# A two-layer outlook-attention kernel: the row shifts of layer 0 move behind the last third of the logits, and some jobs move by a slot

## The chip, the cores and the metric

The kernel runs on one core of one Trainium2 chip. The metric is the device time of one execution in microseconds (us). About 0.3% of it, some 10 us, can be told from no change.

## What is computed

The input `x` is [8, 56, 56, 384] in float32: 8 images of 56 x 56 positions with 384 channels. Two layers follow each other, each of the form x + conv(group_norm(x)). Cut to what matters, layer 0 is:

```python
v = einsum('bhwc,oc->bhwo', x, Wv)                       # values
a = einsum('bhwc,oc->bhwo', x, Wa).reshape(b, n, 12, 9, 9)
attn = softmax(a * 32 ** -0.5, axis=-1)                  # 12 heads, 9 x 9 weights a position
out = einsum('bnhpq,bnqhd->bnphd', attn, v_unf)          # v_unf: the 3 x 3 neighbours of v
...                                                      # each of the 9 outputs is added to its
y = canvas[:, pad:pad + h, pad:pad + w]                  # own neighbour position
return einsum('bhwc,oc->bhwo', y, Wo)
```

Layer 1 is simpler: 6 heads, one set of 9 weights a head and position (with biases), a softmax over the 9, the weighted sum over the 3 x 3 neighbours, and an output projection.

## The kernel before, in words

Images go in pairs (4 pairs, 112 rows of two images side by side on the partitions), and within a pair by image columns (56). Layer 0 runs one column a step, 4 x 56 = 224 steps and 3 more to drain. The instruction order on every engine is written by hand: what Python emits first runs first on its engine.

A step of `layer0` calls `attend(pair, c, between)`. It multiplies the normalised tokens by the attention weights in three thirds (`project`, PSUM tiles called `bank`, TensorE); after each third VectorE takes the maximum (`mx`) and subtracts it (into `at`), and then `between(n)` is called with n = 0, 1, 2. After the thirds come the exponential on ScalarE, the projection to the values `v` (TensorE, copied out by ScalarE) and `between(3)`. The 8 columns of a block are packed into 7 full tiles of 128 tokens; so in every eighth step (step % 8 == 7, where `j == NTILE`) there are no logits, and `attend` only calls `between(0)` to `between(3)`, one after another.

`between` is where all else of the step is put:

- `turning`: TensorE transposes of the next pair's input (`pt`), a ScalarE copy and VectorE statistics.
- `weigh()`: for the column before, the softmax sums on VectorE and the division on POOL (`at<-at,den`); for the column before that, `presum`, which adds the overlapping weights of three neighbouring columns into `pre` (POOL, and two ScalarE copies at n = 3); then the values go to a table in HBM (`vtab`, POOL's DMA queue). In the block's last steps `share_out` spreads the eighth column's weights over DMAs (`last<-at`, `at<-last`, `at<-at`).
- `folding`: `fold` for the column three steps back, in two parts. The first part prepares weight tiles `wts`: VectorE memsets, two ScalarE scalings for each of one or two patches, two TensorE matmuls with a shift matrix (`pw<-pre,shift`), which move rows of `pre` up and down, and a VectorE addition of `pw` and `pre` into `wts` for each patch. The second part issues two DMAs a patch on SyncE (`ztab<-wts`) that write `wts` to a table in HBM.
- `jobs.run(step, 1)`: takes one job from a queue, if the head of the queue is due.

The jobs are made by `fetch`, once in 7 steps for a patch of 7 columns: it loads the table of weights into `z` (one tile for each of the two images, SyncE) and adds ten jobs with the due step `step + 4`: four contractions (two for each image: each does 48 matmuls of a 121-row table with 32 columns, PSUM tile `pc` in two buffers, and ScalarE copies them to `yT`), and six output projections (`po`, one PSUM buffer; VectorE adds the residual into `x1t`). For the last patch of a pair three more jobs follow, the parts of `norm_params` for layer 1: `bn_aggr` on VectorE, the group means (`pgmean`, TensorE), the group variances (`pgvar`). The queue is first in, first out, and a job that is not yet due holds back all behind it. Jobs run at n = 0 and n = 2, and in every eighth step at n = 3 too.

SyncE's DMA queue is in order as well: in a step it holds the table writes of `fold`, then (from `upkeep`) `xT<-xt`, `xr<-in_x`, `xin<-xT`, then (from `flush`) `last<-at`, `at<-last`, `x<-x1t`, `xres<-xT`, and then `vp<-vtab` and `z<-ztab` of `fetch_v` and `fetch`.

The helpers `matmul` and `InOrder` emit every operation, so the profile shows L119 for matmuls, L122 for transposes and L134 for most others; the tile names tell them apart.

Of the kernel before, what the change touches and what calls it, by code (L numbers as in the profile page):

```python
# [15 lines left out]
def two_outlook_layers(  # L16
# [101 lines left out]
    def matmul(*args, **kwargs):  # L118
        tc.keep_in_program_order(nc.tensor.matmul(*args, **kwargs))  # L119
# [26 lines left out]
    def projected(name):  # L146
        return patch.tile([P, NCH, PX, IMG, H], F32, tag="yT", name=f"yT_{name}", bufs=1)
# [195 lines left out]
    def bands(queue, z, table, line, slot, row, top, groups, b, py, npy):  # L343

        for (s0, s1), (m0, m1) in groups:
            first = (b * H + top) * line + s0 * slot + m0 * row
            queue.dma_start(
                z[s0:s1, :, m0 * row : m1 * row],
                bass.AP(
                    table.tensor, table.offset + first + bands.at[row],  # L350
                    [[slot, s1 - s0], [py * line, npy], [1, (m1 - m0) * row]],
                ),
            )
# [19 lines left out]
    NC = 2  # L373
# [10 lines left out]
    jobs = Jobs()  # L384
    later = []

    def flush():
        while later:
            later.pop(0)()
# [21 lines left out]
    def project_half(po, w, yT, half, j):  # L411
        lo, hi = HALVES[half]
        for i in range(NCH):
            matmul(
                po[:, : (hi - lo) * R],
                w[:, i, j * P : (j + 1) * P],
                yT[:, i, lo:hi].rearrange("p m b y -> p (m b y)"),
                start=(i == 0), stop=(i == NCH - 1),
            )

    def layer0(late, pools):
# [342 lines left out]
        def load_res(pair, px):  # L764

            xres[pair, px] = late_w.tile([P, NCH, T], F32, tag="xres", name=f"xres_{pair}_{px}")
            later.append(
                lambda: sync.dma_start(xres[pair, px], xTs[pair][:, :, px * T : (px + 1) * T])
            )

        def fetch(pair, px, due):

            nm = f"0_{pair}_{px}"
            n_tile = 2
            yT = projected(nm)
            if not pair and not px:
                load_res(0, 0)
            for b in range(IMG):
                z, vp = zs[b], vps[b]
                bands(  # L780
                    sync, z, ztab0[(pair * NPX + px) % NTAB], LINE0, SLOT0, ROW0, 0, GROUPS0,
                    b, PY0, NPY0,
                )

                def contract(t, b=b, z=z, vp=vp):
                    pc = ps.tile([P, NCH, n_tile, PY0, PX], F32, tag="c", name=f"pc_{nm}_{b}_{t}", bufs=NC)
                    for n in range(n_tile):
                        py = t * n_tile + n
                        zp = z[: SX0 * SY0, py].rearrange("s (y h m) -> s y h m", y=PY0, h=HEADS0)
                        for h in range(HEADS0):  # L790
                            i, j = divmod(h, P // D0)
                            matmul(
                                pc[j * D0 : (j + 1) * D0, i, n],
                                vp[: SX0 * SY0, py, h * D0 : (h + 1) * D0],
                                zp[:, :, h, :],
                                start=True, stop=True,
                            )
                    rows_of = slice(t * n_tile * PY0, (t + 1) * n_tile * PY0)
                    scalar.copy(
                        yT[:, :, :, b, rows_of], pc.rearrange("p i n y m -> p i m (n y)")  # L800
                    )

                for t in range(0, NPY0 // n_tile, NC):
                    jobs.add(due, lambda t=t, f=contract: [f(t + n) for n in range(NC)])
            if pair == NPAIR - 1 and px == NPX - 1:
                jobs.add(due, clear_bands)
            if px == 0:
                st1s[pair] = stat.tile([P, NCH, IMG, 2 * NPX, 6], F32, tag="st1", name=f"st1_{pair}")

            def project_out(half, j):  # L810
                lo, hi = HALVES[half]
                n = (hi - lo) * R
                po = ps.tile([P, 4 * R], F32, tag="o", name=f"po_{nm}_{half}_{j}")
                project_half(po, wo_t, yT, half, j)
                if j == 0:
                    fetch.x1t = late_w.tile([P, NCH, 4, R], F32, tag="x1t", name=f"x1t_{nm}_{half}", bufs=2)
                x1t = fetch.x1t
                vector.tensor_tensor(
                    x1t[:, j].rearrange("p m r -> p (m r)")[:, :n], po[:, :n],
                    xres[pair, px][:, j, lo * R : hi * R], ALU.add,  # L820
                )
                for b in range(IMG):
                    vector.bn_stats(
                        st1s[pair][:, j, b, 2 * px + half, :],
                        x1t[:, j, : hi - lo, b * H : (b + 1) * H],
                    )
                if j == NCH - 1:
                    later.append(
                        lambda: sync.dma_start(
                            x1s[pair][px, :, :, lo * R : hi * R],  # L830
                            x1t.rearrange("p i m r -> p i (m r)")[:, :, :n],
                        )
                    )
                    if half:
                        del xres[pair, px]
                        following = divmod(pair * NPX + px + 1, NPX)
                        if following[0] < NPAIR:
                            load_res(*following)

            for half in range(2):  # L840
                for j in range(NCH):
                    jobs.add(due, lambda half=half, j=j: project_out(half, j))
            if px == NPX - 1:
                def params_part(n):
                    if n == 0:
                        making["1"] = norm_params(st1s.pop(pair), f"1_{pair}", params1, pair)
                    next(making["1"])

                for n in range(3):
                    jobs.add(due, lambda n=n: params_part(n))  # L850

        making = {}
        clearing = list(clears())
# [47 lines left out]
        for step in range(NPAIR * W + LAG):  # L901
            folding = fold(*divmod(step - LAG, W)) if step >= LAG else iter(())
            turning = turned(step)
            summing = []

            def weigh():

                normal = 1 <= step < NPAIR * W + 1 and (step - 1) % SB < NTILE
                if normal:
                    normalise(*divmod(step - 1, W))  # L910
                if normal and step % SB == NTILE:
                    share_out(*divmod(step - 1, W))
                if 2 <= step < NPAIR * W + 2:
                    summing.append(presum(*divmod(step - 2, W)))
                    next(summing[0])
                if normal and step % SB < NTILE:
                    share_out(*divmod(step - 1, W))
                if normal:
                    keep_v(*divmod(step - 1, W))

            def between(n):

                if n == 0:
                    next(turning, None)
                    weigh()
                    jobs.run(step, 1)
                elif n == 1:
                    next(folding, None)
                    next(turning, None)
                elif n == 2:  # L930
                    jobs.run(step, 1)
                else:
                    for part in summing:
                        next(part)
                    next(folding, None)
                    if step % SB == NTILE:
                        jobs.run(step, 1)

            if step < NPAIR * W:
                attend(*divmod(step, W), between)  # L940
                upkeep(step)
            else:
                for n in range(K + 1):
                    between(n)
            flush()

            pair, c = divmod(step - LAG - PX, W)
            if pair >= 0 and c % PX == 0:
                fetch_v(pair, c // PX)
            pair, c = divmod(step - LAG - PX - 1, W)  # L950
            if pair >= 0 and c % PX == 0:
                fetch(pair, c // PX, step + 4)
# [336 lines left out]
```

## Time and profile before

| | |
|---|---|
| median of 4 runs | 3481.6 us (3475.37 to 3491.45) |
| the profiled execution | 3475.37 us |
| its span, first to last instruction | 3473.5 us |
| TensorE busy, instructions | 3228.6 us, 28510 |
| layer 0 | about the first 2260 us |
| mean granted TensorE clock | 0.965 |
| DMA | 859.13 MB, mean 247 GB/s |

The profile has these views: the busy time of each engine over the span, and in stretches of it (with the granted clock of TensorE and the share of time that the 16 DMA engines were busy); the waits, which say for each engine what it was idle before and whose work ended that idleness; and the timeline of instructions. In a timeline line the number after the start is the duration, x6 is the number of instructions that ran without a gap, and the bracket gives the idle time before the group and what ended it. A float32 matmul stands as two instructions. "issue" is a wait whose end no semaphore in the profile explains.

### The profile page before, as it was taken

To read this page: it belongs to the slowest core of one execution; us is meant where nothing else is said; L and a number is where in the kernel's file an instruction comes from. 1 tells how busy PE (TensorE), PEld (TensorE's weight loads), DVE (VectorE), ACT (ScalarE), POOL (GpSimd) and SP (SyncE) were. 2 spreads that over 40 slices of the span, in tenths; PEclk is the share of its full clock that TensorE was granted. 3 is DMA by queue.
4 is the path that set the end of the run, shared out by engine and by line. 5 is a ranking of instruction groups with operands and counts; after the bars stand their busy time and mean duration, and the time that the engine had idled before them with its cause. 6 is when DMAs were issued, how large, how long until landed. Compare 5 with 4: busy or idle time off the path is not lost.

```text
span 3473.5 us, 74347 instructions
## 1 busy us (share of the span) xinstructions
PE 3228.6 (93%) x28510; PEld 2202.3 (63%) x28510; DVE 1872.6 (54%) x4780; ACT 1368.6 (39%) x3755; POOL 1366.9 (39%) x1982
## 2 busy tenths in 40 slices
PE   7688999999999999999999999888999999999998
PEld 5456676666666666667666666645666666666665
DVE  5556766676777676676666767532333333333231
ACT  4333444344444344443433443323434333433432
POOL 2544545555445454455454555422222222222220
PEclk7899999999999999999999999989999999999998
DMA  6788988888888787879766868768787878787875
GB/s 194 225 286 288 317 278 267 278 277 268 295 278 284 231 278 265 290 260 309 246 198 219 297 227 270 259 225 225 209 227 213 235 212 229 216 221 217 230 211 141
DMA packets 595753, 859.13 MB, mean 247 GB/s; under 512 B 205798, under 2 KB 470950, under 8 KB 591302
## 3 DMA queue, kind: packets, MB, share of 16 engines
q1 hardware_dynamic: 476806, 682.87, 62.4%
q0 software_dynamic: 59136, 148.12, 13.4%
q10 hardware_dynamic: 59456, 23.40, 2.9%
q8 instruction: 224, 3.67, 0.5%
q14 instruction: 131, 1.07, 0.1%
HBM read 520.28 MB, written 330.40 MB: 245 GB/s over the span
## 4 chain that ended last, share of the span: by engine, by line
PE 36%; DMA 7%; issue 3%; DVE 2%; ACT 1%; POOL 1%; SPq 1%; POOLq 0%; DVEq 0%; ACTq 0%
PE bank L119 18%; PE po L119 10%; PE pc L119 5%; DMA at<-lgtab 3%; DMA lgtab<-lgt 1%; DMA ztab<-wts 1%; PE pw L119 1%; PE pt L122 1%; ACT xn L134 1%; PE bank L122 1%; SPq L134 1%; DMA z<-ztab 1%; DMA vtab<-v 0%; POOL at L134 0%; DMA vp<-vtab 0%
## 5 line engine op out<-in xcount | busy, mean ns | idle before, releaser
L119 PE MATMUL bank<-wa_t,xn 128*128 128x288 f32 x3528 | 983.1, 417 | 9.2 <-ACT xn L134 6.1
L119 PE MATMUL po<-yT,wo_t 128*128 128x448 f32 (+1 forms) x2304 | 828.0, 499 | 26.2 <-DVE x1t L134 23.6
L134 POOL TENSOR_TENSOR at<-at,den 128x972 f32<-128x972 f32 x196 | 440.3, 2247 | 930.2 <-DVE den L134 533.9
L119 PEld LDWEIGHTS bank<-wa_t,xn 128*128 128x128 f32 x3528 | 658.8, 194 | 225.7 <-issue 26.2
L119 PEld LDWEIGHTS po<-yT,wo_t 128*128 128x128 f32 x2304 | 429.2, 192 | 316.2 <-issue 188.2
L134 ACT ACTIVATE at<-at 128x972 f32<-128x972 f32 (+1 forms) x228 | 215.3, 944 | 974.0 <-DVE at L134 973.0
L332 POOL DMA_DIRECT2D vtab<-v x392 | 213.1, 547 | 844.1 <-DVE v L134 799.0
L119 PE MATMUL bank<-wc_t,xn 128*128 128x438 f32 x1176 | 480.8, 545 | 0.0
L134 DVE TENSOR_REDUCE mx<-bank 128x36 f32<-128x324 f32 x588 | 284.9, 484 | 350.3 <-PE bank L119 346.8
L119 PE MATMUL pc<-z,vp 121*32 121x49 f32 (+1 forms) x17664 | 385.5, 221 | 62.8 <-ACT yT L134 28.9
L119 PEld LDWEIGHTS pc<-z,vp 121*32 121x32 f32 (+1 forms) x17664 | 346.3, 123 | 133.8 <-issue 84.0
L119 PE MATMUL bank<-wv_t,xn 128*128 128x384 f32 x1176 | 423.7, 497 | 0.0
L134 DVE TENSOR_TENSOR at<-bank,mx 128x324 f32<-128x324 f32 x588 | 291.3, 495 | 170.1 <-ACT pre L134 59.1
L119 PEld LDWEIGHTS bank<-wc_t,xn 128*128 128x128 f32 x1176 | 215.3, 192 | 170.5 <-issue 163.8
L119 PEld LDWEIGHTS bank<-wv_t,xn 128*128 128x128 f32 x1176 | 222.8, 193 | 137.2 <-issue 15.3
L134 POOL DMA_DIRECT2D vtab<-v x476 | 289.5, 612 | 21.8 <-DMA vtab<-zeros 11.1
L134 ACT COPY yT<-pc 128x294 f32<-128x294 f32 (+2 forms) x512 | 196.4, 405 | 244.6 <-PE pc L119 242.8
L134 POOL TENSOR_TENSOR pre<-at,at 112x108 f32<-112x108 f32 (+1 forms) x440 | 224.1, 526 | 92.6 <-DMA at<-last 62.0
L134 DVE SCALAR_TENSOR_TENSOR x1t<-po,bo_t,x1t 128x448 f32<-128x448 f32 (+1 forms) x156 | 97.6, 626 | 249.0 <-PE po L119 249.0
L134 DVE TENSOR_TENSOR lgt<-bank,ba_t 128x54 f32<-128x54 f32 x196 | 41.7, 213 | 348.0 <-PE bank L119 348.0
L134 ACT COPY ot<-pt 112x384 f32<-112x384 f32 x128 | 61.3, 479 | 382.2 <-PE pt L122 341.5
L134 ACT ACTIVATE xn<-xin,bias,scale 128x168 f32<-128x168 f32 (+1 forms) x474 | 208.4, 504 | 3.1 <-DMA xin<-xT 3.1
(113 smaller groups left out, 3075.3 us busy)
## 6 DMA issues: line engine op xcount, KB each, us to landing
z<-ztab SPq DMA_DIRECT2D x64, 2352.0 KB
vp<-vtab SPq DMA_DIRECT2D x64, 1536.0 KB
vp<-vtab SPq DMA_DIRECT2D x64, 945.0 KB
xres<-xT SPq DMA_DIRECT2D x32, 1176.0 KB
ztab<-wts SPq DMA_DIRECT2D x336, 110.2 KB
vtab<-v POOLq DMA_DIRECT2D x108, 336.0 KB, 6.3
xin<-xT SPq DMA_DIRECT2D x52, 672.0 KB
xr<-in_x SPq DMA_DIRECT2D x50, 672.0 KB
```

Of the source, the lines that this page charges most:

```text
L119: tc.keep_in_program_order(nc.tensor.matmul(*args, **kwargs))
L122: tc.keep_in_program_order(nc.tensor.transpose(*args, **kwargs))
L134: return lambda *args, **kwargs: tc.keep_in_program_order(op(*args, **kwargs))
L332: queue.dma_start(bass.AP(table.tensor, table.offset + first, [*([line * step, count] for step, count in rows_of or ((1, rows),)), *([[(R ...
```

## The change

```diff
                 for t in range(0, NPY0 // n_tile, NC):
-                    jobs.add(due, lambda t=t, f=contract: [f(t + n) for n in range(NC)])
+                    jobs.add(due + b, lambda t=t, f=contract: [f(t + n) for n in range(NC)])
...
                 for n in range(3):
                     jobs.add(due, lambda n=n: params_part(n))
+                    if n < 2:
+                        jobs.add(due, lambda: None)
...
                 elif n == 1:
-                    next(folding, None)
                     next(turning, None)
                 elif n == 2:
                     jobs.run(step, 1)
+                    next(folding, None)
```

Three edits, all in layer 0. The first part of `fold` is emitted in `between(2)` after the job instead of at the start of `between(1)`: behind the last third of the logits and the second job of the step. The contractions of the second image (b = 1) become due one step later than those of the first. And between the three parts of `norm_params` for layer 1 an empty job takes a slot each. No instruction is added or removed; only the order on the engines changes.

## The prediction

> **What bounds the kernel now.** I read the busy shares first. TensorE (PE) is busy for 93% of the span and VectorE, the next engine, for 54%, so a microsecond counts only if TensorE gets it back.
>
> ```profile
> PE 3228.6 (93%) x28510; PEld 2202.3 (63%) x28510; DVE 1872.6 (54%) x4780; ACT 1368.6 (39%) x3755; POOL 1366.9 (39%) x1982
> ```
>
> Then the busy time by stages: layer 0 after its start (440 to 2224 us), one step without a stall, and two stretches with one. The columns are us, busy time of PE, PEld, DVE, ACT and POOL, the granted TensorE clock, and the DMA share with GB/s.
>
> ```profile
> 440.00:2224.00 1784.00, 1695.31 (x16423) 1205.11 (x16422) 1230.29 (x3251) 739.59 (x1986) 898.15 (x1208) 0.98 0.80 264
> 638.80:648.70 9.90, 9.90 (x221) 7.41 (x220) 5.70 (x14) 5.25 (x13) 5.48 (x9) 1.00 0.68 219
> 704.30:717.30 13.00, 10.47 (x133) 7.42 (x128) 3.97 (x12) 5.26 (x15) 6.95 (x12) 0.87 0.92 290
> 1318.00:1336.00 18.00, 12.62 (x354) 10.15 (x355) 7.71 (x23) 7.71 (x23) 12.00 (x19) 0.72 0.80 242
> ```
>
> A normal step keeps TensorE busy throughout at full clock. Idle in the long stretch is 1784.0 - 1695.3 = 88.7 us. What ended it is in TensorE's waits of that stretch (total us, times, longest):
>
> ```profile
> PE pw L119 <- POOL pre L134: 26.4, 10, 3.7
> PE po L119 <- DVE x1t L134: 17.7, 20, 4.0
> PE pc L119 <- issue: 13.5, 13, 2.8
> PE pw L119 <- issue: 9.1, 8, 2.4
> PE pc L119 <- ACT yT L134: 5.7, 5, 1.5
> PE pgmean L119 <- DVE mv L134: 5.6, 6, 1.6
> ```
>
> `pw` is the row shift that the change moves. TensorE's timeline shows where it stalls: in the step after one whose number leaves 7 when divided by 8 (a "boundary step", without logits of its own).
>
> ```profile
> 624.52 0.64 PE L119 MATMUL pw<-pre,shift 112*112 112x120 f32 x4 [0.98 <-issue]
> 625.00 3.18 PE L119 MATMUL bank<-wa_t,xn 128*128 128x288 f32 x12
> 631.89 1.14 PE L119 MATMUL pw<-pre,shift 112*112 112x120 f32 x4 [3.71 <-POOL pre L134]
> 632.83 2.69 PE L119 MATMUL bank<-wa_t,xn 128*128 128x288 f32 x6
> 637.29 1.62 PE L119 MATMUL bank<-wa_t,xn 128*128 128x288 f32 x6
> ```
>
> The reader sees two thirds of logits, a stall of 3.71 us, and then the last third at 2.69 us where the same six instructions take 1.62 otherwise. A stall costs its length and a slow stretch behind it. In a normal step `pre` is finished long before: at 600.7 for the `pw` at 607.8.
>
> **Part 1, the row shift behind the last third and the job.** Nothing is added; 224 folds move. On TensorE each `pw` (4 instructions, 0.58 us) now has 6 logits instructions (1.63 us) ahead of it and, where there is a job, a contraction job (1.45 us) or a projection (1.86 to 2.42 us). The stall shrinks by that cover.
>
> Of the ten waits (26.4 us) the trace puts three (2.48, 2.49, 2.85) into boundary steps without logits or jobs: they stay. Three of 3.7 us are in steps without a job: 1.63 us each is covered, 4.9 us. Four (2.53, 0.96, 2.86, 1.03) have third and job in front, 3.1 us or more: 7.4 us goes. Of the eight waits on "issue" one of 1.1 us stands in a full step and goes; the others are in boundary steps. Sum **13.4 us**. The waits before 440 us (9.06 and 3.24 us the largest) I cost at nothing: TensorE waits there for input as well (11.06 us for `xr` at 317), and what is saved is waited for again.
>
> In a boundary step two jobs become neighbours that had `pw` between them. The second waits for the copy or addition that empties the first one's PSUM, as before, but 0.58 us of `pw` no longer fills that wait. With projections, twelve such waits grow by 0.58 us; the 0.58 us then stands between the second and the third job, where about sixteen waits of some 0.6 us are. I set this at zero (between -9 and +7 us).
>
> **Part 2, second image a step later.** Jobs run two a step and three in a boundary step, so only four windows, whose due step is 15, 71, 127 or 183, change: there the third contraction of that step leaves. Two of those thirds stalled 2.65 us (at 1331.7) and 2.81 us (at 1877), behind ScalarE's copies that wait for POOL. Gain 5.5 us, less 4 x 0.6 us of `pw` now uncovered: **3.1 us**. The contraction itself moves, at no cost.
>
> **Part 3, an empty job after two of the three parts of the norm's parameters.** The group means wait for six `bn_aggr` of 0.53 us; one job slot more (about 5 us) covers them. Three of the four windows lie in layer 0; the rows say 5.6 us plus 1.7 us for the variances. I take **5 us**. The fourth is followed by a wait of 11.3 us for `vp` and counts for nothing. The window has 15 job slots in 7 steps and needs 15, so nothing runs over.
>
> **Part 4, the clock.** A row first: 704.3 to 717.3 has 13 us at 0.87, that is 1.7 us lost after a stall of 2.53 us; 1318 to 1336 loses 18 x 0.28 = 5.0 us. Eleven half-clock stretches stand behind the stalls of parts 1 to 3, 24 us together. Some stalls only shrink, so I take half, **12 us** (0 to 24).
>
> The Trainium skill, "TensorE: Matmul & The Clock Gate", section "Part 1: The HAM clock gate", gives half clock after at least one idle window of about 3.4 us. By it only the three stalls of 3.7 us would trip the gate and, cut to 2.1 us, would stop doing so: three times 1.7, or 5 us, and the sum would be 7 us less. The trace disagrees: the clock fell after 2.53 us of idleness.
>
> **What it costs.** The fold's VectorE adds (0.5 us each) now stand behind the last third's reduction and subtraction (0.49 and 0.49 us) and the job's addition and statistics. In the step of 607 us they ran at 610.7 and would run near 613.8; in the contraction step of 641 us, 1.3 us later. VectorE has room (5.70 us busy of 9.90). But SyncE sits on exactly these adds:
>
> ```profile
> SPq L134 <- DVE wts L134: 469.9, 93, 11.9
> ```
>
> So the two table writes and all that is queued behind them on SyncE start 1.3 to 3 us later: `last<-at`, `x<-x1t`, `xin`, `xr`, `xres`, and `z`. Two of these matter. VectorE waits for `last<-at` ten times (48.6 us), because an `at` buffer is still being read; half of those lie behind 500 us, and one shows through on TensorE as 1.44 us for a bank. Five waits longer by 1.5 us: 8 us. And `z`: from the trace's 2,352-byte packets, the first 1,024 of each 2,048 taken as image 0's, the first contraction starts 1.2 to 16.3 us after them, median about 11; five of the 32 windows have 3.6 us or less. About 1 us each: 4 us. Cost **12 us**, between 0 (all hidden) and 62 (below). ScalarE's two to four scalings (0.6 to 1.0 us together) now come just before the exponential; VectorE needs that a step later, so nothing.
>
> **Sum.** 13.4 + 3.1 + 5 + 12 - 12 = 21.5 us. The profiled execution took 3475.4 us (span 3473.5): 3453.9. The median of the four runs is 6.2 us above the profiled one, which was the fastest; I add that: **3460 us**, 0.6% faster.
>
> **Rivals.**
> *Absorbed.* `pre` is late because POOL is, and what TensorE saves it waits for at the next late thing: `last<-at`, `z`, or the x1t addition (17.7 us now). For it: the stalls before 440 us end in waits for transfers. Against it: TensorE is busy for all of a normal step, and POOL for little over half. Then only parts 2 and 3 stay, 8 us less the 12: about 3480 us.
> *SyncE becomes the bound (slower).* The table writes start 3 us later, SyncE is in order, and `last<-at` and `z` land 3 us later in a queue that is busy to 0.80. If that reaches TensorE in full, ten waits for `at` buffers and five tight `z` windows grow by 3 us, 45 us, and ten of them trip the clock, 17 us: 62 us against a gain of 33.5, so 3510 us; with half of it on TensorE about 3480. It decides from a shift of 3 us, where the tight windows' slack ends. For it: SyncE's 469.9 us. Against it: most windows have over 8 us.
> *More than I count.* All 24 us of the clock come back and SyncE's shift is hidden: 45.5 us, 3436 us; with the early stalls too, 3425.
>
> **How the numbers follow.** Measurement tells 0.3%, about 10 us, from no change. My forecast and its neighbourhood (3445 to 3471) 0.45, more than I count 0.21, absorbed 0.18, SyncE slower 0.16. The likeliest is the forecast, 3460. Faster by over 0.3% is the first two, 0.66; within it 0.18; slower 0.16. The range takes in the larger gain and half of the slower rival: 3422 to 3494.
>
> **What would show it.** Right: the `pw` waits on `pre` between 440 and 2224 fall from 26.4 us to 10 to 15, those left standing in boundary steps and behind them; the two long waits of `pc` go; `pgmean` no longer waits for `mv`; the layer's clock rises from 0.98. Wrong: waits of `bank` for `at`, of `pc` for `z` or of `po` for `x1t` grow by as much, or VectorE's wait for `last<-at` rises well above 48.6 us. A fold that becomes late for `z` in most windows would make the prediction wrong in sign.

## The result and the profile after

The changed kernel takes 3487.84 us (median of 53 runs, 3473.67 to 3503.5) against 3479.78 us for the kernel before (79 runs, 3467.59 to 3493.93). The ratio is 1.0025, 95% interval 1.0018 to 1.0032: slower by 0.25%, where 0.6% faster was predicted. Its profiled execution has a span of 3474.2 us, 0.7 us above that of before. The medians differ by 8.1 us, so one profile of each cannot carry the sign; what it can carry is where the stalls went.

Layer 0 by stages in after, with the columns of the prediction's table. The stretch reaches the same step as the one shown of before, and is 14 us longer:

```profile
440.00:2238.00 1798.00, 1698.61 (x16434) 1211.37 (x16429) 1250.63 (x3254) 742.43 (x1991) 901.92 (x1212) 0.98 0.80 263
```

TensorE's idle time is 1798.0 - 1698.6 = 99.4 us; before it was 88.7 us. The clock is the same 0.98. TensorE's waits of after in this stretch (total us, times, longest):

```profile
PE pc L119 <- ACT yT L134: 15.9, 11, 3.5
...
PE pt L122 <- DMA xr<-in_x: 11.0, 5, 3.5
PE pw L119 <- POOL pre L134: 9.6, 4, 2.8
PE bank L119 <- DVE at L134: 8.6, 6, 2.3
PE pw L119 <- ACT pre L134: 7.4, 5, 2.2
```

Read this list against the one of before. The row shift did what was hoped: `pw` waited 26.4 + 9.1 = 35.5 us and now waits 9.6 + 7.4 and, in two smaller rows, 1.0 + 0.9, together 18.9 us. But other rows grew. `pc<-ACT yT` went from 5.7 to 15.9 us. `pt<-DMA xr` went from 2.5 to 11.0 and `bank<-DVE at` from 2.5 to 8.6. Those three alone give back 24.8 us for the 16.6 saved.

The stall that the prediction showed at 631.9 us stands in TensorE's timeline of after here:

```profile
628.00 4.64 PE L119 MATMUL bank<-wa_t,xn 128*128 128x288 f32 x18
634.89 1.14 PE L119 MATMUL pw<-pre,shift 112*112 112x120 f32 x4 [2.25 <-POOL pre L134]
635.82 3.31 PE L119 MATMUL bank<-wv_t,xn 128*128 128x384 f32 x6
```

The last third now runs without a gap behind the first two (18 instructions in one group), and the stall is 2.25 us instead of 3.71. The slow stretch behind it remains: the values' projection takes 3.31 us, elsewhere 2.10. The stall got shorter, but the clock still fell (0.76 granted from 633 to 640 us).

What the fold's lateness does is seen in the waits of the other engines, over the whole run of after:

```profile
DVE at L134 <- DMA last<-at: 91.4, 22, 13.9
...
ACT xn L134 <- DMA xin<-xT: 18.3, 5, 4.8
```

And SyncE's own waits in after:

```profile
SPq L134 <- DVE wts L134: 637.0, 117, 11.0
```

Before, the first was 48.6 us (10 times), the second 3.1 us (once) and the third 469.9 us (93 times). SyncE stands longer in front of `wts`. Relative to the step, its DMAs start later than before by a median of 2.1 us (`ztab`), 2.0 (`last<-at`), 2.5 (`xr`), 1.4 (`z`) and 2.5 (`vp`). `xin` is hardly late at the median (under 0.4 us); it is late in single steps.

### The profile page after: what moved, and what is told of

Its sections match the earlier page's. It is cut to its first block, busy times and chain, and to the rows that moved or that the text cites. A ratio compares the mean times of both kernels' runs of the same rounds, so it can differ in the third digit from the quotient of the medians.

```text
span 3474.2 us, 74310 instructions
## 1 busy us (share of the span) xinstructions
PE 3218.7 (93%) x28510; PEld 2202.4 (63%) x28510; DVE 1894.3 (55%) x4780; ACT 1370.6 (39%) x3755; POOL 1366.5 (39%) x1982
## 3 DMA queue, kind: packets, MB, share of 16 engines
q1 hardware_dynamic: 476806, 682.87, 62.7%
## 5 line engine op out<-in xcount | busy, mean ns | idle before, releaser
L119 PE MATMUL bank<-wa_t,xn 128*128 128x288 f32 x3528 | 943.3, 415 | 14.8 <-DVE at L134 8.2
L119 PEld LDWEIGHTS bank<-wa_t,xn 128*128 128x128 f32 x3528 | 671.9, 194 | 248.6 <-issue 25.5
L134 DVE TENSOR_TENSOR at<-bank,mx 128x324 f32<-128x324 f32 x588 | 291.3, 495 | 197.8 <-DMA last<-at 91.4
L134 POOL DMA_DIRECT2D vtab<-v x476 | 289.5, 612 | 23.0 <-DMA vtab<-zeros 12.3
L119 PEld LDWEIGHTS bank<-wv_t,xn 128*128 128x128 f32 x1176 | 213.2, 195 | 110.7 <-issue 7.0
L134 DVE TENSOR_TENSOR lgt<-bank,ba_t 128x54 f32<-128x54 f32 x196 | 41.6, 212 | 343.8 <-PE bank L119 343.7
L134 ACT ACTIVATE xn<-xin,bias,scale 128x168 f32<-128x168 f32 (+1 forms) x474 | 208.4, 504 | 18.3 <-DMA xin<-xT 18.3
```

The lines of the kernel that those rows point to most:

```text
L134: return lambda *args, **kwargs: tc.keep_in_program_order(op(*args, **kwargs))
```

## The experiments

Three theories were told apart. **S**: the late tables hold SyncE, and what waits in its queue comes too late. **N**: `pw` used to lie between two jobs and covered the second one's wait for its PSUM tile; now it doesn't. A third place for the loss is the other two parts of the change. All ratios are to the kernel before on the same chip, with 95% intervals. The runs are spread over four chips: e1 to e4 on one, e6 to e9 on a second, e10 to e12, the control and e15 on a third, l1, l2, e13 and e14 on a fourth. Where two kernels of different chips are compared, only their ratios are.

### The three parts, one at a time

`e1_fold` is the fold's move alone.

```diff
                 elif n == 1:
-                    next(folding, None)
                     next(turning, None)
                 elif n == 2:
                     jobs.run(step, 1)
+                    next(folding, None)
```

> The fold's first part behind the last third and the job, alone. Theory S (SyncE is in order and sits on the fold's VectorE adds, so tables and all loads and stores behind them start some 2 us later): 0.1 to 0.5% slower than before, VectorE's wait for last<-at near the 91 us of the changed kernel (before 48.6). Rival P (the row shift's place alone pays, and one of the other two edits loses): 0.5% or more faster.

Measured: 1.0063 (1.0038 to 1.0089), 3487.17 us where the kernel before ran 3459.84. Waits of its whole run:

```profile
DVE at L134 <- DMA last<-at: 76.3, 15, 13.5
...
PE pc L119 <- ACT yT L134: 62.7, 30, 5.2
...
ACT xn L134 <- DMA xin<-xT: 18.0, 5, 5.0
```

The same rows as in after are long, and SyncE's wait for `wts` is 667.4 us. The loss sits in this part.

`e2_due` has only `jobs.add(due + b, ...)` for the contractions.

> The second image's contractions due a step later, alone. S and P's first form: within 0.15% of before, since four windows change; the waits of the third contraction in a boundary step (2.65 and 2.81 us) go. If this edit loses by itself: over 0.2% slower.

Measured: 0.9999 (0.9977 to 1.0021). Alone, this edit has no effect that can be measured.

`e3_params` has only the empty jobs:

```diff
                     jobs.add(due, lambda n=n: params_part(n))
+                    if n < 2:
+                        jobs.add(due, lambda: None)
```

> The two empty jobs between the parts of the norm's parameters, alone. My sum: 5 us (0.15%) faster, no wait of pgmean left. After the changed trace: the group means now come right behind the transposes, whose PSUM tile they share, and wait for the copy xt (5.0 and 4.9 us), so 0 to 0.2% slower.

Measured: 1.0009 (0.9990 to 1.0029). The wait for `mv` that the prediction wanted to remove is gone (`pgmean` for `mv`: 8.0 to 0.4 us over the run), but `pgmean` now waits 6.9 and `pgvar` 5.0 us for ScalarE's `xt`. TensorE's timeline of after shows the same:

```profile
773.79 0.55 PE L122 MATMUL pt<-ident,xr 112*128 112x112 f32 x4
777.43 2.50 PE L119 MATMUL pgmean<-mv,gmat 128*128 128x2 f32 x14 [3.09 <-ACT xt L134]
790.72 2.16 PE L119 MATMUL pgvar<-part,gmat 128*128 128x2 f32 x14 [2.45 <-ACT xt L134]
```

The empty jobs shift `pgmean` and `pgvar` to slots at n = 0. There they stand right behind the transposes `pt`, whose PSUM tile they share, and wait 3.09 and 2.45 us for ScalarE's copy `xt` to empty it. Part 3 traded one wait for another.

The three ratios multiply to 1.0071, the whole change has 1.0025. The intervals of the three together reach to about 0.004 either way, so whether the parts help each other is not settled. The kernel before ran at 3459.84 us on the chip of these runs, 0.6% under its time on the others; whether the fold's move costs more there than elsewhere isn't settled either.

### The second part of the fold

`e4_tables_last` is after with the table writes moved behind the step's other SyncE DMAs, so that no `ztab` stands ahead of `last<-at` and `xin`.

```diff
                     for part in summing:
                         next(part)
-                    next(folding, None)
...
             flush()
+            next(folding, None)
```

> The changed kernel, with the fold's table writes issued on SyncE at the end of the step, behind the step's other loads and stores (still ahead of vp and z). S: VectorE's wait for last<-at falls from 91 to under 50 us, ScalarE's for xin from 18 to under 5, and the time to 0.4 to 1% below before (3445 to 3465). P, or ScalarE's scalings as the cause: unchanged within 0.2% of the changed kernel (3480 to 3492).

Measured: 1.0143 (1.0117 to 1.0170), the second largest ratio of all. Its waits:

```profile
ACT wts L134 <- DMA ztab<-wts: 169.2, 47, 17.6
...
DVE at L134 <- DMA last<-at: 43.7, 14, 13.3
```

The wait for `last<-at` halved (91.4 to 43.7 us) and ScalarE's for `xin` fell from 18.3 to 0.8, as S says, but the time that S expected did not follow. The table writes now left so late that the `wts` buffers were still being read when the next fold wanted them: ScalarE's wait for them went from 17 us in after to 169.2 and VectorE's from 7 to 101.7. The order in one queue can't be mended by exchanging who is late.

### Lateness without the moved row shift

`e6_late_adds` keeps `pw` at its old place and only puts VectorE's additions into `wts` behind the second job. That is S without N.

```diff
+            yield   # ahead of the additions in fold
...
                 elif n == 2:
                     jobs.run(step, 1)
+                    next(folding, None)
```

> The kernel before, with only the fold's VectorE additions (the ones that add pw and pre) moved behind the second job; the row shift on TensorE and ScalarE's scalings stay where they were. Theory S (late table writes hold up SyncE): 0.2 to 0.6% slower, VectorE's wait for last<-at 65 us or more, ScalarE waits for xin. Theory N (the row shift no longer stands between the two jobs of a boundary step, and that is the loss): within 0.15% of before.

Measured: 1.0064 (1.0040 to 1.0087). Its waits:

```profile
DVE at L134 <- DMA last<-at: 95.4, 21, 14.3
...
PE pw L119 <- POOL pre L134: 49.7, 19, 11.0
...
ACT xn L134 <- DMA xin<-xT: 16.0, 5, 5.2
```

And the same rows in a control, the unchanged kernel (`c_before`, with run e10 below):

```profile
DVE at L134 <- DMA last<-at: 54.1, 12, 12.5
...
PE pw L119 <- POOL pre L134: 51.0, 17, 9.1
...
ACT xn L134 <- DMA xin<-xT: 5.3, 1, 5.3
```

The `pw` stalls are as before, nothing is gained, and the two waits for transfers have grown to what they are in after (91.4 and 18.3 us), SyncE's for `wts` from 456.2 to 667.3 us. Lateness of the additions alone costs 0.64%, as much as the whole fold's move (0.63%). Since e1 also saves `pw` stalls (24.2 us on POOL against 49.7) and its ratio is no better, what it saves there is spent elsewhere. The row that is longer in e1 is `pc<-ACT yT` on TensorE, 62.7 us against 38.8.

`e7_before_job` puts the fold behind the last third, but ahead of the job (`next(folding, None)` before `jobs.run(step, 1)` at n = 2).

> The fold's first part behind the last third, but ahead of the second job. In boundary steps the row shift stands between the two jobs again. N: 0.3 to 0.6% faster than before, as the stalls of the row shift shrink by 1.63 us each. S: table writes are late by about a third, so about 1 us: between 0.2% faster and 0.3% slower.

Measured: 0.9995 (0.9977 to 1.0014). Standing one job earlier removes the whole loss. VectorE's wait for `last<-at` is long here too (82.2 us), so that wait by itself isn't what costs; ScalarE's for `xin` is 9.1 us.

`e8_not_in_boundary` is e1, except that in boundary steps (where two jobs would become neighbours) the fold stays in front. `e9_after_boundary_only` moves the fold only in the step after a boundary step, where the stalls of 3.7 us were.

```diff
# e8
                 elif n == 1:
+                    if step % SB == NTILE:
                         next(folding, None)
...
# e9
                 elif n == 1:
+                    if step % SB:
                         next(folding, None)
```

> The fold's first part behind the second job in all steps but the boundary ones, where it stays ahead. N: 0.2 to 0.6% faster than before, no waits of pc of over 2.5 us in boundary steps. S: 0.3 to 0.6% slower, as with the fold's move alone (1.0063).

> The fold's first part behind the second job only in the step after a boundary step (28 of 224), where the stalls of 2.5 to 3.7 us were; early everywhere else. S and N both: the covered stalls (some 13 us and part of their clock) without the costs, 0.2 to 0.6% faster than before. If it isn't faster, the stall only moves, whatever SyncE does.

Measured: e8 1.0048 (1.0026 to 1.0069), e9 1.0021 (1.0003 to 1.0039). In e8 the row shift is back between the jobs of the boundary steps, and most of the loss remains, so N is small: 0.15% between the ratios of e1 and e8, inside both intervals. e9 is the surprise: 28 late folds, all where the large stalls are, and it still doesn't win. A table of its steps (from ScalarE's copy of `v` in one step to that of the next) showed why. Its three largest losses against the control are 5.2, 3.75 and 5.7 us at steps 29, 85 and 141, each 56 steps from the next, and at the fourth of this series, 197, it loses 1.2 us. (The next largest, 3.3 and 3.0 us, are at steps 48 and 51.) The four are the first contraction steps of the windows that load their tables right behind a late fold, at steps 24, 80, 136 and 192 (`vp`), with `z` one step later.

### The mechanism in the timeline

That led to one window of this series, the one contracted from step 85 on, in after (which loses 3.9 us at that step) and before. SyncE's queue in after:

```profile
897.29 1.77 SPq L134 DMA_DIRECT2D ztab<-wts  x4
...
906.38 1.08 SPq L134 DMA_DIRECT2D z<-ztab  x2
...
915.74 2.21 SPq L134 DMA_DIRECT2D xin<-xT  x1
```

The same DMAs in the trace of before:

```profile
885.95 1.80 SPq L134 DMA_DIRECT2D ztab<-wts  x4
...
892.73 1.00 SPq L134 DMA_DIRECT2D z<-ztab  x2
902.32 1.01 SPq L134 DMA_DIRECT2D xin<-xT  x1
```

Steps 81 to 84 lie 8.8 to 6.7 us later in after anyway; `z` goes out 13.65 us later, at the end of step 81, so some 5 us later within its step. The packet records say what follows: the 2,048 packets of `z` (2,352 bytes each) start from 907.4 to 922.5 us, over 15.1 us, and the 1,792-byte packets of the two transfers of transposed input behind them (`xT<-xt` and `xin`) come only at the end and after, 921.7 to 926.5. Before, the packets of `z` started from 893.8 to 908.4, and those behind them from 907.0 to 913.3. Then ScalarE in after:

```profile
927.07 1.59 ACT L134 ACTIVATE xn<-xin,bias,scale 128x168 f32<-128x168 f32 x4 [3.97 <-DMA xin<-xT]
...
928.98 0.69 ACT L134 COPY yT<-pc 128x294 f32<-128x294 f32 x2
```

and TensorE in after:

```profile
929.43 1.44 PE L119 MATMUL pc<-z,vp 121*32 121x49 f32 x96 [2.75 <-ACT yT L134]
```

Read the three together from the bottom. The contraction at 929.43 waits 2.75 us for `yT`. ScalarE copies `yT` at 928.98 because it is in order and stood 3.97 us at `xn`. And `xn` stood for `xin`, which was behind `z` in SyncE's queue. The row that grows on TensorE (`pc<-ACT yT`) thus has nothing in common with the thing that was moved but the queue. In before, `xn` of this step runs without a wait, and no contraction of it waits longer than 0.5 us:

```profile
916.30 1.59 ACT L134 ACTIVATE xn<-xin,bias,scale 128x168 f32<-128x168 f32 x4
```

The same chain stands three more times in after, each 56 steps from the next: at 369 us (ScalarE waits 3.85 us for `xin`, then TensorE 2.88 for `yT`), at 1480 (4.76 and 3.53) and at 2015 (1.10 and 1.16). Together TensorE waits 10.3 us in the four; in before there is none.

### Another queue, an earlier fold, a lighter load

`e10_fold_act_queue` is e1 with `last<-at` and `xin<-xT` issued on ScalarE's queue (`scalar.dma_start` for `sync.dma_start`); `e11_before_act_queue` has the same on the kernel before.

> The fold's move alone, with last<-at and xin issued on ScalarE's DMA queue in place of SyncE's. If SyncE's order does the damage (theory S): VectorE's wait for last<-at and ScalarE's for xin fall back to those of the kernel before or under, and the ratio to the next kernel is 1.000 or under. If the late table writes do it through z alone, or the row shift's place itself: 0.4 to 0.7% above the next kernel.

> The kernel before with the same two transfers on ScalarE's queue. S: 0 to 0.4% faster than before. Rival (ScalarE pays for the issues, 0.6 us each): 0 to 0.5% slower.

> The kernel before, unchanged, for its trace and the width of the comparison on this chip: ratio 1.000 within 0.2%.

Measured: e10 1.0182 (1.0153 to 1.0211), e11 1.0062 (1.0040 to 1.0084), the control 1.0005 (0.9986 to 1.0023). The relief failed. VectorE's wait for `last<-at` and ScalarE's of `xn` for `xin` are gone in e10, but TensorE's wait for `xr` is 100.6 us (control 41.6, e11 59.2), and SyncE's for `wts` 750.1. The fold costs 1.2% there (1.0182 / 1.0062), twice as much as in e1. ScalarE, in order too, is held by the issues: its idle time on "issue" is 21.0 us in e11 and 28.5 in e10 (control 3.3), and in e10 the issues of `xin` and `last<-at` at 922.96 and 923.56 us take 0.56 and 0.59 us. S had said 1.000 or under for this pair, so by what was put down it missed; since the queue change has a price of its own, the miss weighs little.

`e12_early` goes the other way: in steps with 2 <= step % 8 < 7 the fold is emitted at n = 0, ahead of `weigh()`.

> The opposite move: the fold's first part before the step's softmax sums and first job, in steps whose number leaves 2 to 6 divided by 8, and as before in the others. Table writes come 1 to 3 us earlier. S: 0.2 to 0.6% faster than before. If lateness only counts in one direction (the slack is enough as it is): within 0.15%; if the row shift now waits for pre: 0.2% or more slower, with over 30 us more of that wait.

Measured: 1.0117 (1.0088 to 1.0147). Its waits:

```profile
PE pw L119 <- POOL pre L134: 83.8, 50, 10.7
...
DVE at L134 <- DMA last<-at: 23.6, 5, 13.3
```

Table writes 1.7 us earlier (median) cut VectorE's wait for `last<-at` from 54.1 to 23.6 us and TensorE's for `xr` from 41.6 to 19.9, which is S seen from the other side. But `pre` isn't ready that early, and `pw` waits 32.8 us more on POOL, and 30.1 us on issue. Put earlier like this, the fold trades one wait for the other.

`l1_light_before` leaves out half of the load of `z` (rows 4 to 7 of each patch aren't loaded and stay zero; the contractions do the same work, and the weighted sums lack half of their rows). `l2_light_fold` is the same with the fold moved as in e1.

```diff
                 bands(
-                    sync, z, ztab0[(pair * NPX + px) % NTAB], LINE0, SLOT0, ROW0, 0, GROUPS0,
-                    b, PY0, NPY0,
+                    sync, z[:, : NPY0 // 2], ztab0[(pair * NPX + px) % NTAB], LINE0, SLOT0, ROW0, 0, GROUPS0,
+                    b, PY0, NPY0 // 2,
                 )
```

> The kernel before with half of every z load of layer 0 left out (rows 4 to 7 of each patch; those stay zero, so the weighted sums lack half of their rows). Its ratio to before is the base for the next kernel: 0.980 to 1.000.

> The fold's move alone with the same half of z left out. If what the late fold loses is lost in the DMA queue behind z (theory Z): its ratio to the light kernel before is 1.000 or under (0.992 to 1.001), against 1.0063 with whole loads, and ScalarE no longer waits for xin. If the loss is in the order of the engines (rival N): 1.004 to 1.008 of the light kernel.

Measured: l1 0.9832 (0.9801 to 0.9862), l2 0.9846 (0.9817 to 0.9875). With the light load the fold's move costs 1.0014 in place of 1.0063, and l2 has no wait for `xin` left. The direction is that of S, but the ratio of the two is known to about 0.4% only, so this pair alone would not decide. And `pc<-ACT yT` still grows, from 32.5 us in l1 to 44.7 in l2. l1 also says that half of the load of `z` is worth 1.7% of the kernel while the engines' work stays the same.

### Not ahead of the loads

If S holds with this place, it suffices to leave the fold early in two steps of seven: those whose end issues `vp` or `z`. `e13_not_before_loads` does so and is e1 otherwise.

```diff
+            loads = (step - LAG - PX) % PX < 2
...
                 elif n == 1:
-                    next(folding, None)
+                    if loads:
+                        next(folding, None)
                     next(turning, None)
                 elif n == 2:
                     jobs.run(step, 1)
+                    if not loads:
+                        next(folding, None)
```

> The fold's first part behind the job in five steps of seven; in the two whose end issues vp or z it stays early. Z: the loss of 0.63% falls to under 0.2%, or turns into 0.1 to 0.4% faster. If last<-at in every step is what counts: 0.3 to 0.6% slower.

Measured: 0.9980 (0.9962 to 0.9999). Its waits:

```profile
DVE at L134 <- DMA last<-at: 50.5, 10, 11.1
...
ACT xn L134 <- DMA xin<-xT: 3.9, 2, 3.0
```

Five sevenths of the folds are late, and both waits are back at the values of before (48.6 and 3.1 us), while `pw` waits 29.6 us on POOL (control 51.0). e13 and e1 differ in nothing but the two steps: these steps cost 1.0063 / 0.9980, or 0.8%. `pc<-ACT yT` is 46.7 us, less than in e1 (62.7) but more than in the control (27.1).

`e14_after_boundary_not_loads` makes the fold late only in the steps after a boundary step that don't issue a load (20 of 28).

```diff
+            late = step % SB == 0 and (step - LAG - PX) % PX > 1
```

> The fold's first part behind the job only in the step after a boundary step, and not where vp or z are issued at its end (20 steps of 224). Z: the stalls that go are not lost again, 0.1 to 0.4% faster than before. If a covered stall always moves on: within 0.1% of before or slower.

Measured: 0.9971 (0.9953 to 0.9990). Against e9, 1.0021, only the eight folds ahead of a load are different, and the sign has turned.

`e15_third_only_not_loads` joins e7 and e13: behind the last third, ahead of the job, and early in the two load steps.

> The fold's first part behind the last third but ahead of the job, and early in the two steps of seven whose end issues vp or z. Theory Z: the small loss that the same place had in all steps (0.9995, where gain and loss cancelled) goes and the gain stays, 0.1 to 0.5% faster. If the loads weren't the cause: 0.9995 again, within 0.15%.

Measured: **0.9940** (0.9919 to 0.9961), 3459.34 us where the kernel before ran 3478.42. Its ratio is below that of every other kernel here with the whole load. The stretch of the same time as that of before, and TensorE's waits in it:

```profile
440.00:2224.00 1784.00, 1694.52 (x16342) 1214.40 (x16340) 1247.39 (x3269) 740.80 (x1990) 910.72 (x1219) 0.98 0.81 267
```

```profile
PE pw L119 <- POOL pre L134: 9.6, 4, 2.8
...
PE pc L119 <- ACT yT L134: 5.0, 5, 1.5
```

TensorE is idle for 89.5 us of it, as in before (88.7), but gets further: ScalarE's last copy of `v` in layer 0 comes at 2216.4 us (before 2232.1, control 2240.7, after 2245.9). The `pw` saving of after on POOL is all there (9.6 us), and `pc<-ACT yT` is at 5.0 us, as before (5.7) and not as after (15.9). e7 differs from it in the same two steps alone, and has 0.9995. VectorE's wait for `last<-at` is still 68.1 us in e15 (control 54.1), and e15 is the fastest all the same.

Three pairs now differ in the load steps alone, e1 and e13, e9 and e14, e7 and e15. Staying early there is better each time, by 0.8, 0.5 and 0.55%, and no two intervals of a pair overlap, though the two kernels of each pair ran on different chips. ScalarE's wait for `xin` falls in each (18.0 to 3.9, 15.8 to 3.3 and 9.1 to 4.5 us), and TensorE's `pc<-ACT yT` with it (62.7 to 46.7, 40.4 to 34.6 and 35.4 to 23.1). That is 16.0, 5.8 and 12.3 us of waiting where the ratios differ by some 29, 17 and 19 us: the chain through `xin` carries a part of what the load steps cost, and how the rest reaches TensorE isn't shown.

The side of the job has a price of its own. e13 and e15 differ only in whether the fold stands behind the job or ahead of it: 0.9980 and 0.9940, with `pc<-ACT yT` at 46.7 and 23.1 us, while ScalarE hardly waits for `xin` in either (3.9 and 4.5 us). What lengthens that row behind the job isn't shown.

## Why the prediction was wrong, step by step

**Part 1, the row shift: mechanism right, size about right.** 13.4 us was predicted for the stretch; the `pw` rows fell by 16.6 us, and the waits on POOL to 9.6 us, just below the 10 to 15 named (7.4 us more are now put down to ScalarE's copies into `pre`). What was left stood in and behind boundary steps, as said. That the size came out so near owes something to luck: single profiles vary by several us, and the place behind the job costs something on `pc<-ACT yT` that the part had left out.

**Part 2, second image a step later: not measurable.** 3.1 us was predicted; alone it measured 0.9999 +- 0.0022, that is 0 +- 8 us. It is neither shown nor excluded. "At no cost" is doubtful: in the window that stalled at 1331.7 us, the fourth contraction waits 2.07 us on "issue" in after, where before it waited 0.39.

**Part 3, the empty jobs: the step failed.** "One job slot more covers them" looked at the `bn_aggr` only and not at the place of the new slot. At n = 0 the group sums stand behind the transposes that hold their PSUM tile. The two rows went from 7.3 to 9.9 us instead of going down by 5.

**Part 4, the clock: nothing came back.** 12 us was predicted. The granted clock of the stretch is 0.98 in both. Adding up the half-clock records of TensorE in it gives 36 us lost before and 41 after. Stalls that shrink to 2.25 us still end in a slow stretch, and new stalls brought slow stretches with them. The 2.25 us of idleness before 634.89 us went with a granted clock of 0.76 from 633 to 640 us and with 3.31 us for 2.10 us of work. The Trainium skill, "TensorE: Matmul & The Clock Gate", section "Part 1: The HAM clock gate", gives half clock after at least one idle window of about 3.4 us; taken as a limit for a single stall, that would have had the stalls cut from 3.7 us keep the full clock, and here they didn't.

**What it costs: this is the step that turned the sign.** The shift of SyncE was right: 1.3 to 3 us were predicted, medians of 1.4 to 2.5 us were measured. The cost of it was mis-sized and sought at the wrong place. e6, lateness alone, costs 0.64%, some 22 us, where 12 us stood in the sum. "Five waits longer by 1.5 us: 8 us" for `last<-at`: VectorE's wait grew by 42.8 us, 12 more times, but TensorE's `bank<-at` by 6.1 only, and e15 is fast with 68.1 us of that wait. "About 1 us each: 4 us" for `z`: the median is about right, but in the window shown it is some 5 us, and TensorE's wait of `pc` for `z` itself grew only from 0.7 to 3.5 us over the run. Part of the loss comes from what stands behind `z`: 15 us of transfer in front of `xin`, then ScalarE in order, then `yT`, then the second contraction. `xin` was named among the things delayed, but no price was put on it. In the stretch TensorE waits 7.4 us right behind ScalarE's waits for `xin`, of the 10.2 by which `pc<-ACT yT` grew, and 8.5 us more for `xr`: 15.9 us on two transfers that had no term in the sum. The argument "most windows have over 8 us" looked at the slack of the load, when the slack of the small load behind it was what mattered in the windows followed here.

With the measured values in place of the five terms the sum is 16.6 + 0 - 2.6 + 0 - 22 = -8 us, as measured (8.1 us slower). It is an estimate from single profiles and one experiment, and that it meets so well is partly luck.

**The rivals.** *SyncE becomes the bound* named the right engine and the right row (637.0 us on `wts`), with a price between 3480 and 3510; 3487.84 lies there. Its mechanism (tight `z` windows) acted little (0.7 to 3.5 us). *Absorbed* would look alike in the time. e6 speaks against it as the main cause: lateness alone, with nothing saved that could be absorbed, costs the full 0.64%, and e15 keeps the saving on `pw` and is faster. *N*, which the prediction had set at zero, is some 0.15% between e1 and e8, inside both intervals; the price of the place behind the job (e13 against e15, 0.4%) is not N alone and had no term.

**What stays open.** In the profiled execution of after, layer 0 ends 14 to 17 us later, but the kernel only 0.7 us: some 11 us return in the first 70 us of layer 1. Why isn't settled. Nor is how 1.0071 for the parts and 1.0025 for the whole go together; e1's 3487.17 us is close to after's 3487.84, and it is the kernel before that was faster on e1's chip. In the window followed, `z` goes out some 5 us late where the table writes ahead of it are about 2.5 late; the rest is a longer gap between `last<-at` and `z` (6.6 us, before 4.2) that no semaphore explains. How the load steps cost more than the waits behind `xin`, and why the place behind the job lengthens `pc<-ACT yT`, is open. Single profiles of the same kernel differ by some 10 us in a step table (control against before: 8.6 us at ScalarE's last copy of `v` in layer 0), so such tables were used only to choose the steps that e13 to e15 then tested.

## What to carry to other kernels

When an instruction is moved back on a full engine, follow not only who waits for its result but the whole in-order queue behind that waiter, and ask of every small load there which large load it will now land behind. A move that is good on average can be spoiled by a few steps: look for the steps where the delayed queue carries a long transfer and leave the old order there (here two of seven, worth 0.5 to 0.8%). A stall removed on the busiest engine counts only if the engines that feed it keep their lead.

## What the runs showed of the hardware

- TensorE's clock halved behind some waits of 1.84 us (ended at 1637.7 in before), 2.25 us (634.9 in after) and 2.53 us (708.6 in before), in stretches of 3.41 us, twice or three times that. Behind other waits no shorter it stayed full: 2.85 us (1786.8 in before) and 2.75 us (929.43 in after), each with 1.00 over the 5 us that followed. So the length of a wait alone did not decide.
- In one queue, 2,048 packets of 2,352 bytes (15 us) hold back a small transfer issued behind them until nearly their end: the last packet of the `xin` issued at 915.74 started at 926.5, and ScalarE went on at 927.07.
- Moving two small DMAs from SyncE's to ScalarE's queue cost 0.6% (e11); ScalarE's idle time on "issue" rose from 3.3 to 21.0 us.
- Chips differ: the kernel before ran at 3459.84 us on one and at 3478 to 3482 on the others, 0.6%, as much as the effects here. Each ratio is therefore to the kernel before on the same chip.
